# One layer of a graph network: 147 columns and 15 rows of a chunk fetched outside the gather queue instead of 35 columns

## The chip, the core and the metric

The kernel runs on one core of one Trainium2 chip. The metric is the device time of one execution in microseconds (us). Five engines run their own instruction streams and meet at semaphores: PE (matrix products into PSUM; its weight loads are listed as PEld), DVE and ACT (element work on 128 partitions), POOL (here it issues the indirect gathers) and SP (here it issues plain DMAs).

## The reference, cut to what matters

```
def reference(x, src, dst, edge_attr_32, W1, b1, W2, b2):     # 12500 nodes x 48, 400000 edges, dst is sorted
    h   = maximum(layernorm(x), 0)
    tmp = concatenate([h[dst], h[src], edge_attr_32], axis=1)   # 400000 x (48 + 48 + 32)
    msg = relu(tmp @ W1 + b1) @ W2 + b2                         # W1: 128 x 128, W2: 128 x 48
    return x + segment_sum(msg, dst, num_segments=12500)
```

## The kernel before

**Tables.** The product `tmp @ W1` is split by the rows of W1. A first stage (`node_tables`) normalises the nodes and writes two tables of 12500 rows of 128 numbers to DRAM: `tab_a` (the part of `h[dst]`, with the bias) and `tab_b` (the part of `h[src]`). A third copy, `bt`, is `tab_b` turned over and kept on chip: 128 partitions, one column for each node.

**Chunks.** The edges are then worked off in chunks of 1024, each of eight tiles of 128 edges: 390 whole chunks and one of five tiles, 391 in all (`NCH`, `T = 8`). Because `dst` is sorted, all destinations of a chunk lie in a window of `W = 80` nodes. For each chunk:

- `prepare` (L353): SP loads one register (L356) and issues three DMAs: the 80 rows of `tab_a` for the window into `rhs` (L359), the edge attributes into rows 80 to 111 of `lhs` (L364), and the destinations, repeated over 80 partitions, into `row` (L366). POOL gathers one row of `tab_b` for every edge, one indirect DMA for each tile of 128 edges, into `gb` (L373; six buffers, so that POOL runs up to six chunks ahead). DVE makes the one-hot matrix of the destinations in `lhs` (L381, which also sums it up along the edges into `deg`), and a second one, `hot`, with edges on partitions (L388).
- `before` (L394): PE makes `pre[t] = lhs[t] x rhs` for the eight tiles, in PSUM. Every product of float32 numbers shows as two matmuls and two weight loads.
- `hidden` (L411): DVE adds `pre` and `gb` into `hid` (L425), ACT applies relu (L432; L431 for a tile that had no gather).
- `fold` (L435): PE sums `hid[t]` by destination with `hot[t]` into `p_g` (L440), and turns `deg` into the second half of `p_g` (L443). `add` (L446) adds `p_g` into the running segment (L455).
- Every twelve chunks the finished segment is multiplied by W2 and stored (L459 to L487).

**Columns.** One tile now and then is not gathered. Its 128 source rows are copied as columns of `bt` into a tile `gt`, one instruction for each edge (`columns`, L340; the copy is L351), and PE adds `gt` turned over into `pre` (`turned`, L406, L409). The column numbers are loaded from `last` into the copying engine's registers ahead of that (`load`, L328; the load shows as TENSOR_LOAD, L316). `PARTS` says how many a chunk gets: three on DVE, two groups of sixteen on ACT. With 35 a chunk, 106 of the 3125 tiles come this way, and 3019 are gathered.

**Order.** The order of the instructions on each engine is written out by hand (`tc.manual_schedule`, L489 to L537): in turn c, `prepare(c)`, `before(c-1)`, `fold(c-2)`, `turned(c-1)`, `hidden(c-1)`, `add(c-2)`, with ACT's first group of columns ahead of its relu and the second behind it.

Of the kernel before, what the change touches and what calls it, by code (L numbers as in the profile page):

```python
# [22 lines left out]
T = 8  # L23
# [25 lines left out]

COLS = 1  # L50
END = NT // T


PARTS = (
    (True, 0, 3, 1),
    (False, 3, 16, 4),
    (False, 19, 16, 20),
)
PART = sum(n for _, _, n, _ in PARTS)
BASE = 36  # L60
DVE_PARTS = sum(dve for dve, *_ in PARTS)
BEHIND = len(PARTS) - 1

BT0 = 16512
SEG0 = 121888
SEG_SIZE = 8 * L


SEG, NEXT, SEG2 = 40, 41, 42
PLACE0 = 43  # L70
WIDTH = 44
SLOTS = (NCH + 2 + P - 1) // P
# [8 lines left out]

BYCOLS = tiles_of(COLS, PART)
TURNED = {c: [j for j, of in enumerate(BYCOLS) if of == c] for c in set(BYCOLS)}

# [4 lines left out]


def gathered_at(c):

    return [t for t in range(min(T, NT - c * T)) if t not in turned_at(c)]

# [153 lines left out]
def windows(nc, tc, gp, bt, ident, idx, x_t, tab_a, tab_b, dst, edge_t, w1, w2s, b2s, out_t):  # L248


    srci, rel, bw, wrow, last, degs = idx
    with ExitStack() as es:
# [19 lines left out]
        for _, _, n, at in PARTS:  # L272
# [3 lines left out]
            )  # L276
        rows_at = slice(BASE, BASE + 1)
        nc.vector.tensor_scalar(
            last[:, :, rows_at], last[:, :, rows_at], 4 * HID, None, op0=ALU.mult
        )  # L280
        taba8 = tab_a.rearrange("n h -> (n h)").bitcast(U8)

# [19 lines left out]
        st = {}  # L302
        gts = {}

        def group(c):
# [17 lines left out]
        def node(n):  # L323
            return n.with_bounds(min_val=0, max_val=N - 1)

        regs = {}
# [26 lines left out]
        def prepare(c):  # L353
            n = min(T, NT - c * T)
            at = c * CE
            base, = numbers(c, BASE, 1, mybir.EngineType.SP)  # L356
            rhs = rhss[c % 3]
            base = base.with_bounds(min_val=0, max_val=4 * HID * (N - 1))
            nc.sync.dma_start(  # L359
                rhs.bitcast(U8)[:W, :],  # L360
                taba8[bass.ds(base, 4 * HID * W)].rearrange("(w h) -> w h", w=W),
            )
            lhs = ld.tile([P, CE], F32, name="lhs")
            nc.sync.dma_start(lhs[W:K, : n * P], edge_t[:, at : at + n * P])  # L364
            row = ld.tile([W, CE], I16, name="row")
            nc.sync.dma_start(  # L366
                row[:, : n * P],
                dst[at : at + n * P].rearrange("(o e) -> o e", o=1).to_broadcast([W, n * P]),
            )
            st[c] = dict(n=n)  # L370
            gb = gp.tile([P, T, HID], F32, name="gb")
            for t in gathered_at(c):
                nc.gpsimd.indirect_dma_start(  # L373
                    out=gb[:, t, :], out_offset=None, in_=tab_b[:, :],
                    in_offset=bass.IndirectOffsetOnAxis(
                        ap=srci[:, c * T + t : c * T + t + 1], axis=0
                    ),
                )

            deg = degs[c % 3]  # L380
            nc.vector.tensor_scalar(  # L381
                lhs[:W, : n * P], row[:, : n * P], bw[:, c : c + 1], None,
                op0=ALU.is_equal, op1=ALU.add, accum_out=deg[:, :1],
            )
            load(c, 0)
            columns(c, 0)
            hot = wp.tile([P, T, W], F32, name="hot")
            nc.vector.tensor_tensor(  # L388
                hot[:, :n, :], wnum.unsqueeze(1).to_broadcast([P, n, W]),
                rel[:, c * T : c * T + n].unsqueeze(2).to_broadcast([P, n, W]), op=ALU.is_equal,  # L390
            )
            st[c].update(rhs=rhs, lhs=lhs, gb=gb, deg=deg, hot=hot)

# [17 lines left out]
        def hidden(c):  # L411
            s = st[c]
            n, pre = s["n"], s["pre"]
            h = wp.tile([P, T, HID], F32, name="hid")
            two = len(turned_at(c)) == 2
# [8 lines left out]
            to = n - len(turned_at(c))  # L424
            nc.vector.tensor_add(added(h, to), added(pre, to), added(s["gb"], to))  # L425
            if two:
                nc.scalar.activation(
                    h[:, half - 1 :: half, :], pre[:, half - 1 :: half, :], AF.Relu
                )
            elif to < n:  # L430
                nc.scalar.activation(h[:, to, :], pre[:, to, :], AF.Relu)  # L431
            nc.scalar.activation(added(h, to), added(h, to), AF.Relu)  # L432
            s["h"] = h

        def fold(c):  # L435
# [3 lines left out]
            for t in range(n):  # L439
                nc.tensor.matmul(  # L440
                    p_g[:, 0, :], s["h"][:, t, :], s["hot"][:, t, :], start=t == 0, stop=t == n - 1
                )
            nc.tensor.matmul(p_g[:, 1, :], s["deg"], ident[:W, :W], start=True, stop=True)  # L443
            s["p_g"] = p_g
# [44 lines left out]
        with tc.manual_schedule():  # L489
            for c in range(NCH + 2):  # L490
                if c < NCH:
                    prepare(c)
                if c >= NCH:
                    load(c, 0)
# [169 lines left out]
def tile_gnn_preln(  # L664
# [54 lines left out]

    degs = []  # L720
    for k in range(3):
        deg = const.tile([W, P], F32, name=f"deg{k}")
        nc.gpsimd.memset(deg, 0.0)
        degs.append(deg)
    gp = ctx.enter_context(tc.tile_pool(name="gp", bufs=6))
# [76 lines left out]
    with tc.If(outside == 0) as cmp:  # L802
        windows(nc, tc, gp, bt, ident, (srci, rel, bw, wrow, last, degs), x_t, tab_a, tab_b, dst16, edge_t,
                w1, w2s, b2s, out_t)
# [70 lines left out]
```

## Time and profile before

| | |
|---|---|
| runs, median (lowest to highest of 3) | 4821.73 us (4817.93 to 4830.65) |
| the profiled execution | 4847.12 us |
| its span, first to last instruction | 4845.3 us |
| instructions in the trace | 55629 |
| granted clock of PE, mean | 0.614 |
| busy: PE, POOL, ACT, DVE | 61%, 60%, 40%, 32% |

How to read it: "busy" counts the engine's own instructions, not its register loads, waits and DMA issues. In the groups of instructions, a row has the line, engine, operation, out<-in by the program's names, shapes, count, busy us and mean ns of one, and then the idle time of the engine just before these instructions with what ended it; "issue" stands for idle time that no wait in the profile explains. The timeline merges neighbours of one kind: start, us from first start to last end, engine, line, and a count.

### The profile page before, as it was taken

To read this page: it belongs to the slowest core of one execution; us is meant where nothing else is said; L and a number is where in the kernel's file an instruction comes from. 1 tells how busy PE (TensorE), PEld (TensorE's weight loads), DVE (VectorE), ACT (ScalarE), POOL (GpSimd) and SP (SyncE) were. 2 spreads that over 40 slices of the span, in tenths; PEclk is the share of its full clock that TensorE was granted. 3 is DMA by queue.
4 is the path that set the end of the run, shared out by engine and by line. 5 is a ranking of instruction groups with operands and counts; after the bars stand their busy time and mean duration, and the time that the engine had idled before them with its cause. 6 is when DMAs were issued, how large, how long until landed. Compare 5 with 4: busy or idle time off the path is not lost. (4 is left out here: it accounts for less than half of the span.)

```text
span 4845.3 us, 55629 instructions
## 1 busy us (share of the span) xinstructions
PE 2962.1 (61%) x14064; PEld 2628.5 (54%) x14064; DVE 1534.8 (32%) x3366; ACT 1944.3 (40%) x12976; POOL 2895.0 (60%) x3047
## 2 busy tenths in 40 slices
PE   5565565555667555665556757666566655665656
PEld 3555564455556555655555656555455555554545
DVE  4333323332333232333323333332233332323333
ACT  3344343443334343443443444343344343434443
POOL 5466565565656566665656666656666665656663
PEclk7756656666555655556656565655655566656566
DMA  3422222222222222222222222222222222222222
GB/s 123 145 72 75 75 71 72 73 73 72 75 68 77 72 73 71 76 73 71 76 71 73 77 73 75 73 71 75 73 72 76 72 74 72 76 69 76 74 71 60
DMA packets 199966, 367.73 MB, mean 76 GB/s; under 512 B 69362, under 2 KB 101636, under 8 KB 198356
## 3 DMA queue, kind: packets, MB, share of 16 engines
q0 software_dynamic: 96640, 198.07, 16.4%
q1 hardware_dynamic: 102736, 165.92, 11.5%
q8 instruction: 115, 1.88, 0.2%
q14 instruction: 215, 1.76, 0.1%
q10 hardware_dynamic: 260, 0.10, 0.0%
HBM read 344.35 MB, written 22.07 MB: 76 GB/s over the span
## 5 line engine op out<-in xcount | busy, mean ns | idle before, releaser
L373 POOL DMA_INDIRECT gb<-tab_b,srci x3019 | 2873.3, 952 | 1898.0 <-DVE seg L455 953.0
L351 ACT COPY gt<-bt 128x1 f32 x12404 | 1495.6, 188 | 1985.4 <-issue 1957.3
L400 PE MATMUL pre<-rhs,lhs 112*128 112x128 f32 x6250 | 1357.6, 386 | 866.3 <-issue 655.1
L400 PEld LDWEIGHTS pre<-rhs,lhs 112*128 112x128 f32 x6250 | 1240.2, 292 | 1052.9 <-issue 849.9
L440 PE MATMUL p_g<-hot,hid 128*128 128x80 f32 x6250 | 1210.5, 366 | 691.2 <-ACT hid L432 312.9
L440 PEld LDWEIGHTS p_g<-hot,hid 128*128 128x128 f32 x6250 | 1156.3, 280 | 742.8 <-ACT hid L432 351.3
L425 DVE TENSOR_TENSOR hid<-pre,gb 128x1024 f32<-128x1024 f32 (+1 forms) x391 | 461.4, 1180 | 1727.0 <-issue 1357.5
L432 ACT ACTIVATE hid<-hid 128x1024 f32<-128x1024 f32 (+1 forms) x391 | 400.3, 1024 | 423.3 <-DVE hid L425 318.2
L381 DVE TENSOR_SCALAR_CACHE_REDUCE lhs<-row,bw 80x1024 f32<-80x1024 int16 x391 | 495.4, 1267 | 9.3 <-DMA row<-in_dst 9.3
L455 DVE TENSOR_TENSOR seg<-seg,p_g 128x160 f32 x391 | 122.4, 313 | 977.1 <-remote 824.1
L388 DVE TENSOR_TENSOR hot<-wnum,rel 128x640 f32<-128x640 f32 x391 | 316.1, 809 | 0.0
L443 PE MATMUL p_g<-ident,deg 80*128 80x80 f32 x782 | 213.4, 356 | 139.1 <-issue 138.8
L443 PEld LDWEIGHTS p_g<-ident,deg 80*128 80x128 f32 x782 | 181.1, 278 | 111.8 <-issue 111.4
L483 DVE TENSOR_TENSOR xseg<-xseg,p_f 48x512 f32<-48x512 f32 (+1 forms) x67 | 45.3, 676 | 497.6 <-remote 291.2
L431 ACT ACTIVATE hid<-pre 128x128 f32<-128x128 f32 x106 | 29.4, 278 | 390.0 <-DVE hid L425 273.8
L409 PE MATMUL pre<-ident,gt 128*128 128x128 f32 x212 | 70.1, 399 | 106.0 <-issue 96.1
L409 PEld LDWEIGHTS pre<-ident,gt 128*128 128x128 f32 x212 | 51.7, 282 | 108.8 <-issue 98.5
L482 PE MATMUL p_f<-seg,b2s 1*48 1x512 f32 (+1 forms) x134 | 98.0, 810 | 11.8 <-issue 11.8
L481 PE MATMUL p_f<-seg,w2s 128*48 128x512 f32 (+1 forms) x134 | 98.0, 815 | 11.3 <-issue 10.0
L351 DVE COPY gt<-bt 128x1 f32 x1164 | 103.0, 141 | 0.0
L482 PEld LDWEIGHTS p_f<-seg,b2s 1*48 1x48 f32 x134 | 13.4, 139 | 92.7 <-issue 91.8
L471 DVE MEMSET seg<- 128x944 f32 x64 | 54.1, 845 | 9.3
(66 smaller groups left out, 327.3 us busy)
## 6 DMA issues: line engine op xcount, KB each, us to landing
row<-in_dst SPq DMA_DIRECT2D x390, 160.0 KB
lhs<-in_edge_t SPq DMA_DIRECT2D x390, 128.0 KB
gb<-tab_b,srci POOLq DMA_INDIRECT x3019
rhs<-tab_a SPq DMA_DIRECT2D x391, 40.0 KB
xseg<-in_x_t SPq DMA_DIRECT2D x33, 192.0 KB
out_x<-xseg SPq DMA_DIRECT2D x33, 192.0 KB
tab_b<-tab SPq DMA_DIRECT2D x3, 1280.0 KB
tab_a<-tab SPq DMA_DIRECT2D x3, 1280.0 KB
```

The lines of the kernel that those rows point to most:

```text
L351: copy(gts[of][:, e : e + 1], bt8[:, bass.ds(at, 4)].bitcast(F32))
L373: nc.gpsimd.indirect_dma_start(out=gb[:, t, :], out_offset=None, in_=tab_b[:, :], in_offset=bass.IndirectOffsetOnAxis(ap=srci[:, c * T + t ...
L381: nc.vector.tensor_scalar(lhs[:W, : n * P], row[:, : n * P], bw[:, c : c + 1], None, op0=ALU.is_equal, op1=ALU.add, accum_out=deg[:, :1],)
L388: nc.vector.tensor_tensor(hot[:, :n, :], wnum.unsqueeze(1).to_broadcast([P, n, W]), rel[:, c * T : c * T + n].unsqueeze(2).to_broadcast([P ...
L400: nc.tensor.matmul(pre[:, t, :], s["lhs"][:K, t * P : (t + 1) * P], s["rhs"][:K, :], start=True, stop=t not in turned_at(c),)
L409: nc.tensor.matmul(st[c]["pre"][:, t, :], gts.pop(j), ident, start=False, stop=True)
L425: nc.vector.tensor_add(added(h, to), added(pre, to), added(s["gb"], to))
L432: nc.scalar.activation(added(h, to), added(h, to), AF.Relu)
L440: nc.tensor.matmul(p_g[:, 0, :], s["h"][:, t, :], s["hot"][:, t, :], start=t == 0, stop=t == n - 1)
L443: nc.tensor.matmul(p_g[:, 1, :], s["deg"], ident[:W, :W], start=True, stop=True)
L455: nc.vector.tensor_add(to, to, s["p_g"])
L482: nc.tensor.matmul(p_f[:, :n], b2s[:1, :], seg[:1, 1, s], start=False, stop=True)
```

## The change

`PARTS` grows from three groups to nine: four on DVE (19, 16, 16 and 20 columns, 71 in all) and five on ACT (16, 16, 16, 16 and 12, 76 in all), each with a register load of its own. In a turn DVE copies 19 columns between the two one-hots, 32 after them, and 20 behind `add`; ACT copies 48 ahead of the relu and 28 behind it. With 147 columns a chunk 446 tiles come by columns, in 57 chunks two of them.

A new path fetches single rows: SP loads fifteen more registers a chunk, and the new function `rows` issues one DMA of one row of `tab_b` (512 bytes) for each, into a tile `gs`; 45 tiles come this way. 2634 tiles are still gathered.

The one-hot at L381 no longer sums along the edges; the degrees come from PE, which multiplies a constant bfloat16 tile (ones in its first column, zeros elsewhere) with the upper halves of the float32 numbers of `hot`, eight products a chunk in place of one of float32. `hidden` adds in place in PSUM (two or three additions in the 45 chunks that have a tile of single rows), and one relu reads all eight tiles from there.

```diff
--- before.py
+++ after.py
@@ -48,27 +48,35 @@
 
 
 COLS = 1
+ROWS0 = 1
 END = NT // T
 
 
 PARTS = (
-    (True, 0, 3, 1),
-    (False, 3, 16, 4),
-    (False, 19, 16, 20),
+    (True, 0, 19, 1),
+    (True, 19, 16, 20),
+    (True, 35, 16, 36),
+    (True, 51, 20, 52),
+    (False, 71, 16, 72),
+    (False, 87, 16, 88),
+    (False, 103, 16, 104),
+    (False, 119, 16, 120),
+    (False, 135, 12, 136),
 )
 PART = sum(n for _, _, n, _ in PARTS)
-BASE = 36
+BASE = 148
+RPART = 15
 DVE_PARTS = sum(dve for dve, *_ in PARTS)
-BEHIND = len(PARTS) - 1
+BEHIND = len(PARTS) - 2
 
 BT0 = 16512
-SEG0 = 121888
+SEG0 = 122592
 SEG_SIZE = 8 * L
 
 
-SEG, NEXT, SEG2 = 40, 41, 42
-PLACE0 = 43
-WIDTH = 44
+SEG, NEXT, SEG2 = 164, 165, 166
+PLACE0 = 167
+WIDTH = 168
 SLOTS = (NCH + 2 + P - 1) // P
 MOST = 32
 
@@ -80,6 +88,7 @@
 
 
 BYCOLS = tiles_of(COLS, PART)
+BYROWS = tiles_of(ROWS0, RPART)
 TURNED = {c: [j for j, of in enumerate(BYCOLS) if of == c] for c in set(BYCOLS)}
 
 
@@ -88,9 +97,14 @@
     return ((), (T - 1,), (T // 2 - 1, T - 1))[len(TURNED.get(c, ()))]
 
 
+def single_at(c):
+
+    return (T - 2 if c in TURNED else T - 1) if c in BYROWS else None
+
+
 def gathered_at(c):
 
-    return [t for t in range(min(T, NT - c * T)) if t not in turned_at(c)]
+    return [t for t in range(min(T, NT - c * T)) if t not in turned_at(c) and t != single_at(c)]
 
 
 EPS = 1e-5
@@ -248,7 +262,7 @@
 def windows(nc, tc, gp, bt, ident, idx, x_t, tab_a, tab_b, dst, edge_t, w1, w2s, b2s, out_t):
 
 
-    srci, rel, bw, wrow, last, degs = idx
+    srci, rel, bw, wrow, last, ones = idx
     with ExitStack() as es:
         seg = es.enter_context(tc.tile_pool(name="segs", bufs=1))
 
@@ -274,11 +288,11 @@
                 last[:, :, at : at + n], last[:, :, at : at + n], 4, BT0,
                 op0=ALU.mult, op1=ALU.add,
             )
-        rows_at = slice(BASE, BASE + 1)
+        rows_at = slice(BASE, BASE + 1 + RPART)
         nc.vector.tensor_scalar(
             last[:, :, rows_at], last[:, :, rows_at], 4 * HID, None, op0=ALU.mult
         )
-        taba8 = tab_a.rearrange("n h -> (n h)").bitcast(U8)
+        tab8, taba8 = (t.rearrange("n h -> (n h)").bitcast(U8) for t in (tab_b, tab_a))
 
         place = PARTS[0][3] - 1
         for a, b in ((place, SEG2), (NEXT, SEG)):
@@ -301,6 +315,7 @@
             rhss.append(rhs)
         st = {}
         gts = {}
+        gss = {}
 
         def group(c):
 
@@ -322,6 +337,19 @@
 
         def node(n):
             return n.with_bounds(min_val=0, max_val=N - 1)
+
+        def rows(c, nodes):
+
+            for k, n in enumerate(nodes):
+                e = (c - ROWS0) * RPART + k
+                of = BYROWS[e // P]
+                if of not in gss:
+                    gss[of] = gtp.tile([P, HID], F32, name="gs")
+                n = n.with_bounds(min_val=0, max_val=4 * HID * (N - 1))
+                nc.sync.dma_start(
+                    gss[of].bitcast(U8)[e % P : e % P + 1, :],
+                    tab8[bass.ds(n, 4 * HID)].rearrange("(o h) -> o h", o=1),
+                )
 
         regs = {}
 
@@ -353,7 +381,8 @@
         def prepare(c):
             n = min(T, NT - c * T)
             at = c * CE
-            base, = numbers(c, BASE, 1, mybir.EngineType.SP)
+            m = max(0, min(RPART, len(BYROWS) * P - (c - ROWS0) * RPART)) if c >= ROWS0 else 0
+            base, *nodes = numbers(c, BASE, 1 + m, mybir.EngineType.SP)
             rhs = rhss[c % 3]
             base = base.with_bounds(min_val=0, max_val=4 * HID * (N - 1))
             nc.sync.dma_start(
@@ -367,7 +396,7 @@
                 row[:, : n * P],
                 dst[at : at + n * P].rearrange("(o e) -> o e", o=1).to_broadcast([W, n * P]),
             )
-            st[c] = dict(n=n)
+            st[c] = dict(n=n, rows=nodes)
             gb = gp.tile([P, T, HID], F32, name="gb")
             for t in gathered_at(c):
                 nc.gpsimd.indirect_dma_start(
@@ -377,10 +406,8 @@
                     ),
                 )
 
-            deg = degs[c % 3]
             nc.vector.tensor_scalar(
-                lhs[:W, : n * P], row[:, : n * P], bw[:, c : c + 1], None,
-                op0=ALU.is_equal, op1=ALU.add, accum_out=deg[:, :1],
+                lhs[:W, : n * P], row[:, : n * P], bw[:, c : c + 1], None, op0=ALU.is_equal,
             )
             load(c, 0)
             columns(c, 0)
@@ -389,7 +416,7 @@
                 hot[:, :n, :], wnum.unsqueeze(1).to_broadcast([P, n, W]),
                 rel[:, c * T : c * T + n].unsqueeze(2).to_broadcast([P, n, W]), op=ALU.is_equal,
             )
-            st[c].update(rhs=rhs, lhs=lhs, gb=gb, deg=deg, hot=hot)
+            st[c].update(rhs=rhs, lhs=lhs, gb=gb, hot=hot)
 
         def before(c):
 
@@ -411,7 +438,6 @@
         def hidden(c):
             s = st[c]
             n, pre = s["n"], s["pre"]
-            h = wp.tile([P, T, HID], F32, name="hid")
             two = len(turned_at(c)) == 2
             half = T // 2
 
@@ -422,14 +448,17 @@
                 return x.rearrange("p (b t) h -> p b t h", b=2)[:, :, : half - 1, :]
 
             to = n - len(turned_at(c))
-            nc.vector.tensor_add(added(h, to), added(pre, to), added(s["gb"], to))
-            if two:
-                nc.scalar.activation(
-                    h[:, half - 1 :: half, :], pre[:, half - 1 :: half, :], AF.Relu
-                )
-            elif to < n:
-                nc.scalar.activation(h[:, to, :], pre[:, to, :], AF.Relu)
-            nc.scalar.activation(added(h, to), added(h, to), AF.Relu)
+            at = single_at(c)
+            if at is None:
+                parts = [(added(pre, to), added(s["gb"], to))]
+            else:
+                runs = [(0, half - 1), (half, at)] if two else [(0, at)]
+                parts = [(pre[:, a:b, :], s["gb"][:, a:b, :]) for a, b in runs]
+                parts.append((pre[:, at, :], gss.pop(c)))
+            for of, rows in parts:
+                nc.vector.tensor_add(of, of, rows)
+            h = wp.tile([P, T, HID], F32, name="hid")
+            nc.scalar.activation(h[:, :n, :], pre[:, :n, :], AF.Relu)
             s["h"] = h
 
         def fold(c):
@@ -440,7 +469,11 @@
                 nc.tensor.matmul(
                     p_g[:, 0, :], s["h"][:, t, :], s["hot"][:, t, :], start=t == 0, stop=t == n - 1
                 )
-            nc.tensor.matmul(p_g[:, 1, :], s["deg"], ident[:W, :W], start=True, stop=True)
+            high = s["hot"].bitcast(BF16)
+            for t in range(n):
+                nc.tensor.matmul(
+                    p_g[:, 1, :], ones, high[:, t, 1::2], start=t == 0, stop=t == n - 1
+                )
             s["p_g"] = p_g
 
         def add(c):
@@ -490,6 +523,7 @@
             for c in range(NCH + 2):
                 if c < NCH:
                     prepare(c)
+                    rows(c, st[c].pop("rows"))
                 if c >= NCH:
                     load(c, 0)
                     columns(c, 0)
@@ -717,11 +751,9 @@
     flag = const.tile([1, 1], I32, name="flag")
     last = const.tile([P, SLOTS, WIDTH], I32, name="last")
 
-    degs = []
-    for k in range(3):
-        deg = const.tile([W, P], F32, name=f"deg{k}")
-        nc.gpsimd.memset(deg, 0.0)
-        degs.append(deg)
+    ones = const.tile([P, P], BF16, name="ones")
+    nc.gpsimd.memset(ones, 0.0)
+    nc.gpsimd.memset(ones[:, :1], 1.0)
     gp = ctx.enter_context(tc.tile_pool(name="gp", bufs=6))
 
     with tc.tile_pool(name="keep", bufs=1) as keep, tc.tile_pool(
@@ -800,7 +832,7 @@
     outside = nc.values_load(flag[:1, :1], min_val=0, max_val=1)
 
     with tc.If(outside == 0) as cmp:
-        windows(nc, tc, gp, bt, ident, (srci, rel, bw, wrow, last, degs), x_t, tab_a, tab_b, dst16, edge_t,
+        windows(nc, tc, gp, bt, ident, (srci, rel, bw, wrow, last, ones), x_t, tab_a, tab_b, dst16, edge_t,
                 w1, w2s, b2s, out_t)
     with cmp.Else():
         general(nc, tc, bt, ident, x_t, tab_a, tab_b, src_it, dst_it, dst, edge_t, w1, w2s, b2s,
@@ -837,6 +869,10 @@
     cols = np.pad(cols, (0, -len(cols) % PART)).reshape(-1, PART)
     for _, k, n, at in PARTS:
         numbers[COLS : COLS + len(cols), at : at + n] = cols[:, k : k + n]
+    in_rows = [c * T + single_at(c) for c in BYROWS]
+    rows = by_tile[in_rows].reshape(-1)
+    rows = np.pad(rows, (0, -len(rows) % RPART)).reshape(-1, RPART)
+    numbers[ROWS0 : ROWS0 + len(rows), BASE + 1 : BASE + 1 + RPART] = rows
     last = np.ascontiguousarray(numbers.reshape(SLOTS, P, WIDTH).transpose(1, 0, 2))
 
     arrays = {
```

## The prediction

> **What bounds the kernel now.** The page comes first, then the groups of instructions with shapes kept apart.
>
> ```profile
> span 4845.3 us, 55629 instructions
> PE 2962.1 (61%) x14064; PEld 2628.5 (54%) x14064; DVE 1534.8 (32%) x3366; ACT 1944.3 (40%) x12976; POOL 2895.0 (60%) x3047
> ...
> L373 POOL DMA_INDIRECT gb<-tab_b,srci x3019 | 2873.3, 952 | 1898.0 <-DVE seg L455 953.0 <-issue 855.9 <-DVE hid L425 52.6
> L351 ACT COPY gt<-bt 128x1 f32 x12404 | 1495.6, 188 | 1985.4 <-issue 1957.3 <-DVE last L290 4.2
> ```
>
> No engine is full. POOL comes nearest: its gathers and the fixed gap behind each take (2873.3 + 855.9) / 3019 = 1.235 us, or 9.54 us a chunk over 391 chunks, and it waits 953.0 / 391 = 2.44 us a chunk for DVE to free a buffer. The first and last addition of `hidden` give the pace:
>
> ```profile
> L425 DVE TENSOR_TENSOR hid<-pre,gb x391: 809/1209/1226, 157.6 to 4832.7; 128x1024 f32<-128x1024 f32 x140, 128x896 f32<-128x896 f32 x55, 128x640 f32<-128x640 f32 x1
> ```
>
> (4832.7 - 157.6) / 390 = 11.99 us a chunk: gathers plus wait, 9.54 + 2.44. So the other engines are not hidden behind POOL; POOL stops for them. Why they are late is in the waits, where the largest sum of all is not a wait for another engine:
>
> ```profile
> ACT gt L351 <- issue: 1957.3, 2796, 1.9
> ```
>
> 2796 times a column copy came 1957.3 / 2796 = 0.70 us late with nothing to wait for. The timeline says when:
>
> ```profile
> 2003.67 2.55 ACT L351 COPY gt<-bt 128x1 f32 x25
> ...
> 2017.75 0.19 ACT L351 COPY gt<-bt 128x1 f32 x1 [1.20 <-issue]
> ...
> 2019.03 0.94 POOL L373 DMA_INDIRECT gb<-tab_b,srci  x1 [0.30 <-issue]
> 2019.15 0.19 ACT L351 COPY gt<-bt 128x1 f32 x1 [1.21 <-issue]
> 2019.17 0.37 PE L400 MATMUL pre<-rhs,lhs 112*128 112x128 f32 x1 [2.41 <-issue]
> 2019.86 0.19 ACT L351 COPY gt<-bt 128x1 f32 x1 [0.52 <-issue]
> ...
> 2020.57 0.37 PE L400 MATMUL pre<-rhs,lhs 112*128 112x128 f32 x1 [1.03 <-issue]
> ...
> 2025.78 0.95 POOL L373 DMA_INDIRECT gb<-tab_b,srci  x1 [4.55 <-DVE seg L455]
> ...
> 4800.69 0.95 POOL L373 DMA_INDIRECT gb<-tab_b,srci  x1 [0.31 <-issue]
> ...
> 4802.58 3.27 ACT L351 COPY gt<-bt 128x1 f32 x32
> ```
>
> While POOL has been gathering for some microseconds, ACT and PE issue one instruction each 0.7 or 1.4 us; once it pauses they run freely, and behind the very last gather (4800.69) ACT makes 32 copies in 3.27 us, 0.102 us each. Two windows cut one cycle, just over two chunks with 15 gathers, into these halves for ACT's copies:
>
> ```profile
> 2006.10:2024.00 17.90, 4.47 (x29) 0.60 0.21 54
> 2024.00:2029.10 5.10, 3.60 (x37) 0.50 0.40 117
> ```
>
> Slow: 29 copies in 17.9 us, 1.62 per us, and 17.9 / 15 = 1.193 us of slow time a gather. Free: 37 copies in 5.1 us. I read the kernel as two phases that take turns: POOL's gathers, in which the others crawl, and its pause, in which they catch up.
>
> The rule must give the present time. With 3019 / 391 = 7.72 gathers a chunk: slow 9.21 us, in it 14.9 copies of the 12404 / 391 = 31.7; the other 16.8 at 0.102 us take 1.71 us; then the relu, which follows them on ACT:
>
> ```profile
> L432 ACT ACTIVATE hid<-hid 128x1024 f32<-128x1024 f32 x284 | 299.7, 1055 | 415.4 <-DVE hid L425 310.3 <-issue 104.8
> ```
>
> 9.21 + 1.71 + 1.06 = 11.98 us, where 11.99 were measured. ACT's column copies fill the pause already now.
>
> **The change, part by part.**
>
> *Gathers.* 2634 instead of 3019, 6.74 a chunk. Slow time 6.74 x 1.193 = 8.04 us, 1.17 us less: a gain of 390 x 1.17 = 456 us.
>
> *ACT's columns.* 76 instead of 31.7. In the slow 8.04 us go 13.0; the other 63.0 take 63.0 x 0.102 = 6.43 us of pause. The 0.102 us holds the register loads, since the 32 copies are two groups of sixteen with their loads. The pause is then 6.43 + 1.06 = 7.49 us, and the chunk 8.04 + 7.49 = **15.53 us**, 3.54 us more than now.
>
> *DVE's columns.* 71 instead of 3, in order with its other work:
>
> ```profile
> 2026.85 0.27 DVE L351 COPY gt<-bt 128x1 f32 x3
> ...
> L425 DVE TENSOR_TENSOR hid<-pre,gb 128x1024 f32<-128x1024 f32 x284 | 345.2, 1216 | 985.9 <-issue 895.6 <-ACT gt L351 50.9 <-remote 39.3
> L381 DVE TENSOR_SCALAR_CACHE_REDUCE lhs<-row,bw 80x1024 f32<-80x1024 int16 x390 | 494.5, 1268 | 9.3 <-DMA row<-in_dst 9.3
> L388 DVE TENSOR_TENSOR hot<-wnum,rel 128x640 f32<-128x640 f32 x390 | 315.6, 809 | 0.0
> L455 DVE TENSOR_TENSOR seg<-seg,p_g 128x160 f32 x391 | 122.4, 313 | 977.1 <-remote 824.1 <-PE pre L400 53.7 <-issue 53.6
> ...
> L351 DVE COPY gt<-bt 128x1 f32 x1164 | 103.0, 141 | 0.0
> ...
> L316 ACTq TENSOR_LOAD <-last x776: 314/1041/2327, 139.6 to 4811.2; - x194
> L316 DVEq TENSOR_LOAD <-last x425: 315/349/770, 155.6 to 4832.4; - x142
> ```
>
> Copies follow each other at (0.27 - 0.14) / 2 = 0.065 us; the large operations take 1.22 + 1.27 + 0.81 + 0.31 = 3.61 us a chunk. How DVE crawls with columns to make no row shows; I take ACT's rate, 13 copies, which leaves 58 x 0.065 = 3.8 us. Four loads of 16 to 20 numbers cost between DVE's 0.349 us (four numbers or one) and ACT's 1.041 us (sixteen) each, 1.4 to 4.2 us, hidden behind queued copies or not. At most half of the large work, 1.8 us, falls into the slow time. DVE's pause thus lies between 3.8 + 3.6 - 1.8 = 5.6 and 3.8 + 3.6 + 4.2 = 11.6 us. Sixteen copies with their load at ACT's pace, 1.63 us, are nearest: 58 / 16 x 1.63 + 3.6 - 1.8 = 7.7 us, level with ACT's 7.5. I add nothing, and keep both ends.
>
> *Rows by SP.* Fifteen more DMAs a chunk and a load of sixteen numbers.
>
> ```profile
> 2003.45 0.33 SPq L359 DMA_DIRECT2D rhs<-tab_a  x1
> 2003.87 0.37 SPq L364 DMA_DIRECT2D lhs<-in_edge_t  x1
> 2004.29 0.46 SPq L366 DMA_DIRECT2D row<-in_dst  x1
> ```
>
> One issue each 0.42 us: 18 x 0.42 + 1.04 = 8.6 us of the 15.5. Queued behind the rows are the next chunk's `rhs`, `lhs` and `row`, on which PE and DVE wait. Cost nothing while SP gets at least part of the slow time; if it got none, 8.04 + 8.6 = 16.6 us, 1.1 us a chunk more.
>
> *Degrees, one-hot, relu.*
>
> ```profile
> 2003.65 3.70 PE L440 MATMUL p_g<-hot,hid 128*128 128x80 f32 x16 [0.24 <-issue]
> ...
> L443 PE MATMUL p_g<-ident,deg 80*128 80x80 f32 x782 | 213.4, 356 | 139.1 <-issue 138.8
> L431 ACT ACTIVATE hid<-pre 128x128 f32<-128x128 f32 x106 | 29.4, 278 | 390.0 <-DVE hid L425 273.8 <-issue 110.6 <-DVE seg L455 5.6
> ```
>
> L381 loses its sum: a gain between 0 and half of its 1.27 us. On PE two matmuls a chunk (782 / 391) go and eight come, and 446 turned tiles instead of 106 add 1.7; at 3.70 / 16 = 0.23 us each as the upper end and nothing as the lower for the eight, PE is between 0.1 us less and 1.8 us more busy a chunk. ACT's longer pause hides that; uncovered it costs 1.8 us. One relu for all tiles saves L431's 29.4 us, below 0.1 us a chunk. The sum in PSUM keeps a buffer of `pre` until ACT's relu has read it, not only until DVE has added; the next user of that buffer on PE, `before` two chunks on, stands behind `fold` of the same chunk, which waits for that relu already, so nothing is queued behind a new wait. I book all of this at zero.
>
> The Trainium skill, "SBUF — State Buffer", section "Who interferes with whom", says that a `tensor_scalar` without an accumulator output may take a two-port mode that locks GpSimd out, which the present form of L381 does not. No run here shows that form. As an estimate from that page, the halved time would take up to 0.6 us a chunk from DVE and could hold POOL as long.
>
> **Sum.** 390 x 15.53 + 157.6 (first addition) + 4845.3 - 4832.7 (what follows the last) = 6227 us of span. The profiled execution is 1.8 us longer than its span (4847.1) and 25.4 us above the median of the runs (4821.7): 6227 + 1.8 - 25.4 = **6200 us**.
>
> **The rivals.**
>
> *Faster: the columns do hide beside the gathers.* If the 0.70 us delays came from these queues having little ready, a queue full of copies would keep its pace through the gathers. A chunk then takes the busiest engine: POOL 6.74 x 1.235 = 8.3 us, ACT 76 x 0.102 + 1.06 = 8.8, SP 8.6, DVE 71 / 16 x 1.63 + 3.6 = 10.8. 390 x 10.8 + 170 - 24 = **4360 us**, 3580 us with DVE's loads hidden and ACT the bound (8.8). It decides at break-even: a chunk of 11.99 us needs 47.7 of the 76 copies in the slow 8.04 us, 5.9 per us instead of 1.62. Against it stand the 2796 delays with nothing waited for, and PE, whose matmuls were ready and crawled alike. The Trainium skill's page "SBUF — State Buffer", same section, takes this side: "PE and ACT never wait on anyone", and a DMA never contends with a compute engine. These rows do not agree with it, unless the cause lies outside that memory. Chance 0.13.
>
> *Milder:* part of the copies use the slow time better, or fewer gathers in a run leave them freer. At 5 per us: 8.04 + 35.8 x 0.102 + 1.06 = 12.75 us, 5120 us. Chance 0.11, for 4900 to 5600 us.
>
> *DVE is the later one:* its loads stand open: 11.6 - 1.8 = 9.8 us of pause, 17.8 us a chunk, **7090 us**. For it: DVE's copies, loads and large operations are one queue, and `hidden` stands behind 51 copies. Chance 0.20, for 6700 to 7600 us. More than that (both ends together, 19.6 us) 0.05.
>
> **How the numbers follow.** The forecast, 5600 to 6700 us around 6200, has 0.51. The range 5000 to 7600 us leaves out the faster rival, a little of the milder one, and the far end, 2 in 10. A difference of 0.3% is about what the runs can tell from none. Slower 0.86, same 0.01, faster 0.13.
>
> **What would show it.** In the changed profile: 2634 gathers still 1.24 us apart; POOL's wait for DVE up from 2.4 to about 7 us a chunk; the delays before ACT's copies still near 0.70 us, now with DVE's copies showing them too; free stretches of some 7 us with ACT at 0.1 us a copy. I am wrong in the mechanism if copies run at 0.1 us through long runs of gathers, and wrong in size if DVE or SP, not ACT, works last in the pauses.

## The result, and the profile after

The changed kernel takes 5369.16 us (median of 4 runs, 5364.9 to 5372.86) where the kernel before, run beside it, takes 4826.19 us: a ratio of 1.1126 with a 95% interval of 1.1105 to 1.1147, 543 us slower. The forecast (6200 us, 1378 us above the kernel before) had the sign and the two phases, at two and a half times the size.

The page of the changed kernel and its groups of instructions:

```profile
span 5368.5 us, 117719 instructions
PE 3296.4 (61%) x17087; PEld 2982.2 (56%) x17087; DVE 3216.3 (60%) x29465; ACT 3501.3 (65%) x29954; POOL 2588.0 (48%) x2661
...
L379 ACT COPY gt<-bt 128x1 f32 x29488 | 3117.8, 188 | 1675.4 <-issue 1645.1
L402 POOL DMA_INDIRECT gb<-tab_b,srci x2634 | 2566.6, 974 | 2712.3 <-DVE pre L459 1794.2 <-issue 704.5 <-DVE seg L488 169.8
L379 DVE COPY gt<-bt 128x1 f32 x27600 | 2039.7, 145 | 1773.3 <-issue 1751.8 <-DMA gs<-tab_b 3.7
```

The chain of work that ended last, by engine (the profile follows it back through the last 40% of the span):

```profile
DVE 21%; issue 14%; DVEq 2%; ACT 2%; PE 1%; SPq 0%; ACTq 0%; DMA 0%
```

Gathers are still (2566.6 + 704.5) / 2634 = 1.242 us apart. POOL's waits for DVE grew from 2.6 to (1794.2 + 169.8) / 391 = 5.0 us a chunk, where the forecast had some 7, and the delays with nothing to wait for now stand in front of DVE's copies too. The chain is DVE's: its addition, behind which POOL's buffer comes free, stands behind its columns. The list of waits adds how often each came (us in total, times, longest):

```profile
DVE gt L379 <- issue: 1751.8, 3086, 1.3
ACT gt L379 <- issue: 1645.1, 2927, 4.2
...
POOL gb L402 <- DVE pre L459: 1794.2, 350, 54.6
...
POOL gb L402 <- DVE seg L488: 169.8, 28, 7.3
```

The same two waits of POOL in the kernel before:

```profile
POOL gb L373 <- DVE seg L455: 953.0, 217, 8.9
...
POOL gb L373 <- DVE hid L425: 52.6, 11, 48.4
```

The counts hold much of the answer, and the forecast had read only the sums. Before, POOL stopped 217 + 11 = 228 times, so a run of gathers was 3019 / 228 = 13.2 long on average, mostly two chunks. After, it stopped 350 + 28 = 378 times: runs of 2634 / 378 = 7.0, one chunk each. The windows of ACT's copies over one cycle of the changed kernel (length, busy time, instructions, granted clock, DMA share, GB/s) show what a short run does:

```profile
2502.40:2509.80 7.40, 6.20 (x63) 0.65 0.26 68
2509.80:2516.00 6.20, 1.92 (x14) 0.60 0.20 53
```

The free stretch is 7.4 us, where the forecast had 7.49 for ACT's pause; but POOL stands still for only 4.61 us of it, and the rest lies beside the first gathers. The slow one is 6.2 us and not 8.04: the timeline has the first of seven gathers at 2506.06, with ACT making 24 copies at full pace beside the second and third, the last at 2513.72, and ACT free again from 2516.02:

```profile
2506.06 0.94 POOL L402 DMA_INDIRECT gb<-tab_b,srci  x1 [4.61 <-DVE pre L459]
...
2507.79 2.31 ACT L379 COPY gt<-bt 128x1 f32 x24
...
2511.76 0.28 ACT L379 COPY gt<-bt 128x1 f32 x2 [1.14 <-issue]
...
2513.72 0.94 POOL L402 DMA_INDIRECT gb<-tab_b,srci  x1 [0.30 <-issue]
...
2516.02 1.02 ACT L379 COPY gt<-bt 128x1 f32 x10 [0.51 <-issue]
```

So the crawl began 2509.80 - 2506.06 = 3.7 us behind the restart and was over at 2516.02. The same delay stood in the cycle from which the forecast took its rate. Its slow window began at 2006.10, and POOL had restarted 3.3 us earlier:

```profile
2002.78 0.94 POOL L373 DMA_INDIRECT gb<-tab_b,srci  x1 [4.61 <-DVE seg L455]
```

In both cycles these free microseconds came once for the run of gathers, whether it had seven or fifteen.

### The profile page after: what moved, and what is told of

It reads as the page before. It is cut to its first block, busy times and chain, and to the rows that moved or that the text cites. A ratio compares the mean times of both kernels' runs of the same rounds, so it can differ in the third digit from the quotient of the medians.

```text
span 5368.5 us, 117719 instructions
## 1 busy us (share of the span) xinstructions
PE 3296.4 (61%) x17087; PEld 2982.2 (56%) x17087; DVE 3216.3 (60%) x29465; ACT 3501.3 (65%) x29954; POOL 2588.0 (48%) x2661
## 5 line engine op out<-in xcount | busy, mean ns | idle before, releaser
L379 ACT COPY gt<-bt 128x1 f32 x29488 | 3117.8, 188 | 1675.4 <-issue 1645.1
L402 POOL DMA_INDIRECT gb<-tab_b,srci x2634 | 2566.6, 974 | 2712.3 <-DVE pre L459 1794.2
L379 DVE COPY gt<-bt 128x1 f32 x27600 | 2039.7, 145 | 1773.3 <-issue 1751.8
L469 PE MATMUL p_g<-hot,hid 128*128 128x80 f32 x6250 | 1420.8, 420 | 1980.7 <-ACT hid L461 1298.9
L461 ACT ACTIVATE hid<-pre 128x1024 f32<-128x1024 f32 x391 | 396.1, 1013 | 95.9 <-DVE pre L459 76.8
L459 DVE TENSOR_TENSOR pre<-pre,gb 128x896 f32<-128x896 f32 (+2 forms) x394 | 412.7, 1047 | 4.1 <-issue 1.9
L436 PE MATMUL pre<-ident,gt 128*128 128x128 f32 x892 | 329.5, 483 | 24.1 <-remote 21.2
L474 PEld LDWEIGHTS <-ones 128*128 128x128 bf16 x3125 | 295.6, 155 | 0.0
L409 DVE TENSOR_SCALAR lhs<-row,bw 80x1024 f32<-80x1024 int16 x391 | 290.0, 742 | 8.3 <-DMA row<-in_dst 8.3
L474 PE MATMUL p_g<-hot,ones 128*128 128x80 bf16 x3125 | 287.0, 267 | 0.0
```

The source lines that it names most:

```text
L379: copy(gts[of][:, e : e + 1], bt8[:, bass.ds(at, 4)].bitcast(F32))
L402: nc.gpsimd.indirect_dma_start(out=gb[:, t, :], out_offset=None, in_=tab_b[:, :], in_offset=bass.IndirectOffsetOnAxis(ap=srci[:, c * T + t ...
L409: nc.vector.tensor_scalar(lhs[:W, : n * P], row[:, : n * P], bw[:, c : c + 1], None, op0=ALU.is_equal,)
L436: nc.tensor.matmul(st[c]["pre"][:, t, :], gts.pop(j), ident, start=False, stop=True)
L459: nc.vector.tensor_add(of, of, rows)
L461: nc.scalar.activation(h[:, :n, :], pre[:, :n, :], AF.Relu)
```

## The experiments

Columns, rows, degrees and gathers were first taken apart; then, since none of them alone explained the size, the gathers' rhythm was changed. Times are medians, and a ratio stands to the kernel before, run beside it (4824 to 4848 us). The code shows what each edit is about; lines that only follow from it (places in `last`, sizes, the filling of the tables) are left out.

**Do gathers cause the crawl?** The same buffers, zeroed once, and no gather at all, in both kernels:

```
-            for t in gathered_at(c):
-                nc.gpsimd.indirect_dma_start(...)
+        gb = gp.tile(...); nc.vector.memset(gb, 0.0)      # once, ahead of the loop
```

> The changed kernel without its 2634 gathers: one buffer of zeros takes the place of gb, all else stays. Two phases (gathers make the other queues crawl, the rest runs in POOL's pauses): the chunk shrinks from 13.3 us to the free part alone, ACT 76 x 0.102 + 1.0 = 8.8 us, DVE with its loads 8 to 10.8 us: 9.5 us a chunk, about 3870 us (3600 to 4400), and the 0.57 us delays before the copies are gone. Rival, DVE and ACT are simply full of small instructions and the gathers do not matter to them: 13 us a chunk, 5000 to 5370 us, delays still there.

> The kernel before without its 3019 gathers, zeros in their place. Two phases: what is left is PE's two rows of sixteen products, 4 to 8 us a chunk by the granted clock, about 6.5 us: 2700 us (1900 to 3300), no 0.70 us delays. Rival (the gathers only occupy POOL): the others' pace of 11 to 12 us a chunk stays, 4400 to 4800 us.

Measured 3538 us for the changed kernel, a little less than expected, and 2029 us for the one before (one run each). ACT's copies in the groups of the kernel before without gathers:

```profile
L353 ACT COPY gt<-bt 128x1 f32 x12404 | 1223.3, 187 | 24.9 <-issue 10.2 <-DVE last L290 4.2
```

10.2 us of delays where there were 1957.3: the crawl is the gathers'. Without them the change costs 1509 us, the work that it adds.

**The columns alone, from the other side.** All 106 column tiles of the kernel before are gathered instead:

```
-    (True, 0, 3, 1), (False, 3, 16, 4), (False, 19, 16, 20),
+    (True, 0, 0, 1), (False, 0, 0, 4), (False, 0, 0, 20),
```

> The kernel before with no columns at all: all 3125 tiles gathered, DVE and ACT copy nothing. Two phases: 8 gathers a chunk, run together as now, slow about 8.7 us, and the pause loses the 16.8 copies that ACT makes in it (1.7 us of 3.6): 10.6 to 11.5 us a chunk, 4300 to 4650 us, faster than before. Rival, POOL is the bound and every tile taken from it pays: 106 more gathers at 1.235 us are 131 us more, 4950 us.

5119.24 us, a ratio of 1.0605 (1.0586 to 1.0624): slower. The first 106 tiles by columns gain 291 us, 2.7 us a tile, more than the 1.235 us that a gather takes of POOL. So the rule that columns are paid in POOL's pause does not hold for the first of them. The chain and the stops say more:

```profile
PE 48%; issue 45%; another core or an unknown queue 4%; DVE 1%; ACT 1%; DMA 0%; DVEq 0%; SPq 0%; ACTq 0%
```

Without any columns PE and its unexplained delays are the chain, and to take ACT's copies away does not shorten the chunk. POOL stopped 129 + 6 times for DVE, so runs were 3125 / 135 = 23 gathers long, against 13 in the kernel before. That fits a cost that grows with the run; what lengthened the runs was not tried.

**The changed kernel with 35 columns**, rows, degrees and relu as changed:

```
-PARTS = ((True, 0, 19, 1), (True, 19, 16, 20), ... (False, 135, 12, 136))
+PARTS = ((True, 0, 3, 1), (False, 3, 16, 4), (False, 19, 16, 20))
```

> The changed kernel with the columns of the kernel before (3 on DVE, 32 on ACT); rows by SP, degrees by PE, the sum in PSUM with one relu and the one-hot without its sum stay. If the columns carry the loss, this is within 2% of the kernel before, 4650 to 4900 us, a little under it for 45 gathers fewer (56 us) and 0.5 us a chunk less on DVE. Rival, the rows by SP or the eight products for the degrees carry a good part: 5050 us or more.

5588.76 us, a ratio of 1.1565 (1.1545 to 1.1585): slower than with 147. The group of the comparison on DVE names the place:

```profile
L403 DVE TENSOR_SCALAR lhs<-row,bw 80x1024 f32<-80x1024 int16 x391 | 299.1, 765 | 2323.4 <-DMA row<-in_dst 2044.3
```

DVE waits 2044 us for the load of `row`, which stands behind the rows on SP. To see each part by itself, four kernels followed.

**Rows alone** in the kernel before, 45 tiles fewer gathered:

```
                     prepare(c)
+                    rows(c, st[c].pop("rows"))
```

> The kernel before with the fifteen rows a chunk by SP and nothing else of the change (45 tiles no longer gathered; 35 columns, degrees and relu as before). Theory now: SP's queue crawls through the fifteen one-row DMAs beside the gathers and holds back the next chunk's `row`, `lhs` and `rhs` behind it; with everything else as before that alone takes 5350 to 5600 us, and DVE waits for the DMA of `row`. Rival (the degrees on PE carry the loss of the 35-column form): the rows cost nothing and save 45 gathers of 1.2 us, 4750 to 4850 us. As on record before the change, the rows would cost nothing.

5638.22 us, a ratio of 1.1678 (1.1631 to 1.1724). The timeline (start, length, queue or engine, operation, count, idle before) of SP and POOL shows why:

```profile
2498.76 0.41 SPq L389 DMA_DIRECT2D row<-in_dst  x1
2499.27 17.43 SPq L343 DMA_DIRECT2D gs<-tab_b  x15
2517.31 0.32 SPq L382 DMA_DIRECT2D rhs<-tab_a  x1
2517.74 0.36 SPq L387 DMA_DIRECT2D lhs<-in_edge_t  x1
2518.14 0.42 SPq L389 DMA_DIRECT2D row<-in_dst  x1
2518.96 4.88 SPq L343 DMA_DIRECT2D gs<-tab_b  x15
...
2513.24 0.95 POOL L396 DMA_INDIRECT gb<-tab_b,srci  x1 [0.30 <-issue]
2524.38 0.95 POOL L396 DMA_INDIRECT gb<-tab_b,srci  x1 [10.19 <-DVE seg L486]
```

Fifteen rows leave in 4.88 us in POOL's pause (2514.2 to 2524.38) and in 17.43 us beside its gathers, and the next chunk's `row` waits behind them; DVE waits 3206 us for it in all. That is 810 us of loss where nothing was booked.

**Degrees alone** in the kernel before:

```
-                op0=ALU.is_equal, op1=ALU.add, accum_out=deg[:, :1],
+                op0=ALU.is_equal,
...
-            nc.tensor.matmul(p_g[:, 1, :], s["deg"], ident[:W, :W], start=True, stop=True)
+            for t in range(n):
+                nc.tensor.matmul(p_g[:, 1, :], ones, high[:, t, 1::2], start=t == 0, stop=t == n - 1)
```

> The kernel before with the degrees by PE from a column of ones (eight bf16 matmuls a chunk instead of two, the comparison of `lhs` without its sum) and nothing else of the change. Theory now (rows carry the loss): within 100 us of the kernel before, 4780 to 4930 us. Rival (PE's sixteen more queued instructions a chunk crawl beside the gathers): 5250 to 5600 us.

4844.34 us, a ratio of 1.0028 (1.0006 to 1.005): as good as nothing, as booked, with each gather a little longer (952 ns before):

```profile
L373 POOL DMA_INDIRECT gb<-tab_b,srci x3019 | 2991.2, 991 | 1781.6 <-DVE seg L457 824.3
```

The delays before ACT's copies fell here from 1957 to 812 us, and ACT waited longer for DVE's addition in their place. The time did not move, so these delays alone are no price.

**147 columns alone** (the kernel before with the `PARTS` of the changed one):

> The kernel before with 147 columns a chunk (71 DVE, 76 ACT) instead of 35 and nothing else of the change: 340 tiles no longer gathered. Going from 0 to 106 tiles by columns brought 2.7 us a tile; in the changed kernel 340 more brought 0.65 us a tile. Theory now (columns gain, rows lose): 4200 to 4650 us, faster. Rival, the theory on record (columns are made in POOL's pause and cost more than their gathers): 5400 us or more.

5207.31 us, a ratio of 1.0782 (1.0765 to 1.08): 379 us, between the two numbers expected, so both theories had it wrong: the columns do lose, and far less than forecast. **The changed kernel without its rows:**

```
-BYROWS = tiles_of(ROWS0, RPART)
+BYROWS = []
```

> The changed kernel without the rows by SP: their 45 tiles are gathered by POOL again, the 147 columns, the degrees on PE and the one relu in PSUM stay. Theory now (rows carry the loss): faster than both, 4250 to 4700 us. Rival (the degrees on PE or the sum in PSUM carry it): 5150 to 5400 us, about as the changed kernel.

5012.31 us, a ratio of 1.0375 (1.0358 to 1.0392), again between the two. With 147 columns alone POOL stopped 333 + 45 times for DVE, so 2679 gathers came in runs of 7.1. With 35 columns and the rest of the change the runs were 2974 / (193 + 40) = 12.8. So it is the 147 columns that cut them. Taken in this order the parts give the change as a sum: before 4828, columns + 379 = 5207, degrees and relu - 195 = 5012, rows + 357 = 5369; alone in the kernel before, degrees and rows cost 16 and 810 us. The 195 us are DVE's for the most part, as far as the profile tells (degrees and relu were not tried apart with 147 columns): the chain has DVE at 51% with the columns alone and at 25% behind that, and the comparison of `lhs` takes 0.58 of its time without its sum. The chain by engine and L387 with the columns alone, then L409 without rows:

```profile
DVE 51%; issue 32%; ACT 9%; DVEq 3%; PE 1%; ACTq 1%; POOL 0%; DMA 0%; POOLq 0%
...
L387 DVE TENSOR_SCALAR_CACHE_REDUCE lhs<-row,bw 80x1024 f32<-80x1024 int16 x391 | 494.5, 1265 | 7.8 <-DMA row<-in_dst 7.8
```

```profile
L409 DVE TENSOR_SCALAR lhs<-row,bw 80x1024 f32<-80x1024 int16 x391 | 289.1, 739 | 8.5 <-DMA row<-in_dst 8.5
```

391 x (1.265 - 0.739) = 206 us. The one relu is busy for 396 us on ACT, where the relus with the columns alone took 470.

**Longer runs of gathers.** If short runs are why the loss was smaller than forecast, long ones must bring it back. One buffer for two chunks, three of them instead of six:

```
-            gb = gp.tile([P, T, HID], F32, name="gb")
+            if c % 2 == 0:
+                pair[0] = gp.tile([P, 2 * T, HID], F32, name="gb")
+            gb = pair[0][:, c % 2 * T : c % 2 * T + T, :]
```

> The changed kernel with one gather buffer for two chunks (three of them instead of six single ones), so that POOL's gathers come in runs of some 14 instead of 6 to 7; nothing else differs. In the traces the others crawl from 3.7 us after POOL restarts to the end of the run, 6.2 us for a run of 7 but 17.6 us for one of 15. Theory (slow time grows faster than the run, so short runs are why the changed kernel lost less than forecast): slow 16.4 us per two chunks, in it some 27 to 37 of ACT's 152 copies, and (152 - 32) x 0.102 + 2.1 = 14.3 us of pause: 30.7 us per two chunks, 5700 to 6200 us. Rival (slow time per gather does not hang on the run): within 100 us of the changed kernel's 5369 us.

6210.17 us, a ratio of 1.2799 (1.2758 to 1.2839), just above the range expected, where the prediction of the change had been 6200. POOL's stops, the delays before ACT's copies in the whole run, and a window of ACT's copies over one run of fourteen and the start of the pause behind it:

```profile
POOL gb L405 <- DVE pre L462: 2714.6, 185, 62.7
ACT gt L380 <- issue: 2391.8, 3094, 4.2
```

```profile
2508.50:2524.50 16.00, 2.76 (x17) 0.72 0.17 50
2524.50:2535.00 10.50, 8.91 (x92) 0.50 0.11 34
```

Runs of 2634 / (185 + 4) = 13.9 (four more stops were for DVE's `seg`), 16.0 us of slow time for one of fourteen (1.14 us a gather against 0.89 in the run of seven; 1.06 copies per us), ACT free behind it. The same 2634 gathers and 29488 copies now come with 2392 us of delays instead of 1645, and POOL waits 2714.6 / 391 = 6.9 us a chunk. The kernel still has its rows, whose fifteen DMAs also meet longer runs here, so the 10 us between 6210 and 6200 say less than the slow time does.

**Shorter runs and wider gaps.** A dummy write of POOL, which nothing reads, behind the fourth tile of a chunk, or behind every gather (no rows in these two):

```
                 nc.gpsimd.indirect_dma_start(out=gb[:, t, :], ...)
+                if t == 3:                          # first kernel
+                    for _ in range(4): nc.gpsimd.memset(idle, 0.0)
+                nc.gpsimd.memset(idle[:, :384], 0.0)   # second kernel
```

> The changed kernel without the rows, and with four dummy writes of 640 numbers by POOL (some 2.4 us) behind the fourth tile of each chunk, which cut a run of seven gathers into two of three or four. Theory (the crawl starts only 3.7 us behind POOL's restart): most of the slow 6 us a chunk goes, 4200 to 4700 us, where the kernel without rows took 5012. Rival (the others crawl whenever gather packets flow): POOL's longer run adds to it, 5000 to 5500 us.

> The changed kernel without the rows, and with one dummy write of 384 numbers by POOL (some 0.4 us) behind every gather: gathers 1.6 instead of 1.24 us apart. Theory A (the crawl is a backlog that gathers build up at their full rate): 4300 to 4800 us. Theory B (the others crawl as long as gather packets flow, at whatever rate): slow time grows with POOL's time by 2.6 us a chunk, 5200 to 5700 us. Without the dummy writes it took 5012 us.

4726.38 us (0.9748, 0.9717 to 0.9778), just outside the range expected, and 4601.32 us (0.949, 0.946 to 0.9519): faster than the kernel before, and 286 and 411 us faster than without the dummy work. The delays before ACT's copies fell from 1374 us to 1087 and 807 us with the same gathers and the same bytes. So a good part of the slowing hangs on gathers following each other at full rate, and not on their being there.

**Fewer columns**, again without rows:

```
+PARTS = ((True, 0, 19, 1), (True, 19, 16, 20), (False, 35, 16, 36), (False, 51, 16, 52))
```

> The changed kernel without the rows and with 67 columns a chunk (35 by DVE, 32 by ACT) instead of 147; degrees on PE and one relu in PSUM stay. Theory (the first columns, made where an engine has nothing else to do, gain; those beyond that lengthen POOL's pause): 4550 to 4800 us, faster than before. Rival (a straight line between the 4844 us of 35 columns with degrees on PE and the 5012 us of 147): 4890 us.

5102.45 us, a ratio of 1.0524 (1.0491 to 1.0558): both numbers missed. Its waits explain it after the fact:

```profile
POOL gb L397 <- DVE seg L483: 875.4, 130, 12.6
...
POOL gb L397 <- DVE pre L454: 440.3, 87, 52.9
```

2922 / (130 + 87) = 13.5: with 67 columns POOL still runs through two chunks at a time, and pays for the columns as well. That its runs are the reason wasn't tried by itself.

**Gaps in the kernels themselves, and their width.** The changed kernel with its rows and 384, the kernel before with 256, and 512 without rows:

```
+                nc.gpsimd.memset(idle[:, :384], 0.0)   # or :256, :512
```

> The changed kernel as it is, with the rows, and with the dummy write of 384 numbers by POOL behind every gather. Theory 1 (what the rows cost, 357 us, is that their queue and the others crawl beside gathers at full rate): with the crawl thinned out the rows cost little, 4500 to 4750 us. Theory 2 (the rows cost by themselves, as fifteen more transfers and their queue time on SP): 357 us more than the 4601 us of the same kernel without rows, 4900 to 5050 us.

> The kernel before with a dummy write of 256 numbers by POOL (some 0.3 us) behind every gather and nothing else. POOL then needs 7.72 x 1.53 = 11.8 us a chunk of the 12.0 it has. Theory (gathers at their full rate build up a backlog that lets all queues crawl): the others keep their pace and POOL bounds the kernel, 4550 to 4780 us, faster. Rival (spacing helps only where an engine has 76 columns to make): 4830 to 5200 us.

> The changed kernel without the rows, with a dummy write of 512 instead of 384 numbers by POOL behind every gather. POOL's own time is then 6.85 x 1.70 = 11.6 us a chunk. Theory (a wider gap takes more of the 807 us of delays before ACT's copies away, and then POOL bounds): 4450 to 4750 us with delays before ACT's copies below 500 us. Rival (the delays that are left do not hang on the gap): delays of about 800 us still, and 4700 to 4900 us.

4559.93 us (0.9448, 0.9422 to 0.9473), 4700.23 us (0.9736, 0.9712 to 0.976) and 4625.62 us (0.958, 0.9558 to 0.9603). The kernel before gains too, so gaps do not pay only where there are many columns. With gaps of 384 the rows no longer cost: 4560 us with them, 4601 without. Their 357 us came with the gathers at full rate. At 512 the crawl is gone and POOL is the bound (the chain by engine, and groups):

```profile
POOL 82%; issue 10%; DVE 4%; PE 2%; DMA 1%; DVEq 0%; ACT 0%; POOLq 0%; SPq 0%; ACTq 0%
...
L403 POOL DMA_INDIRECT gb<-tab_b,srci x2679 | 2611.4, 975 | 464.1 <-issue 438.5
L380 ACT COPY gt<-bt 128x1 f32 x29488 | 2889.3, 187 | 102.9 <-issue 40.5
...
L409 POOL MEMSET idle<- 1x512 f32 x2679 | 1462.9, 546 | 42.2 <-DMA tab_a<-tab 42.2
```

**Is it the transfers or the indirect form?** In the kernel before, each gather becomes a plain load of 128 neighbouring rows on POOL's queue:

```
-                nc.gpsimd.indirect_dma_start(out=gb[:, t, :], in_=tab_b[:, :], in_offset=...)
+                nc.gpsimd.dma_start(gb[:, t, :], tab_b[at_t : at_t + P, :])
```

> The kernel before with each gather replaced by a plain load of 128 neighbouring rows on the same queue of POOL, same bytes into the same buffer; the sums over edges are then of other rows. Theory A (the crawl comes from transfers of POOL's queue following each other at full rate, indirect or not): POOL's issues stay near 1 us each and the kernel near 4500 to 5000 us, with the 0.7 us delays before ACT's copies. Theory B (it comes from the indirect form): no such delays, 2000 to 3500 us.

2013 us (one run). Its page:

```profile
q0 software_dynamic: 96640, 198.07, 35.1%
...
L374 POOL DMA_DIRECT2D gb<-tab_b x3019 | 1592.8, 536 | 345.4 <-DVE seg L451 166.7
L351 ACT COPY gt<-bt 128x1 f32 x12404 | 1223.3, 187 | 25.4 <-issue 10.0
```

The same 3019 transfers and 198 MB, each issued in 536 instead of 952 ns, and 10.0 us of delays. So neither the bytes nor the number of transfers on POOL's queue make the crawl. Whether the making of an indirect transfer does it or its scattered rows isn't told apart by this run.

**The version that beats both**, the changed kernel with 448, and one step past it, with 179 columns and 480:

```
+                nc.gpsimd.memset(idle[:, :448], 0.0)   # or :480
```

> The changed kernel as it is, with the rows, and with a dummy write of 448 numbers by POOL behind every gather, between the 384 (4560 us, ACT bound with 802 us of delays) and the 512 (4626 us without rows, POOL bound with 40 us of delays). POOL's own time is 6.74 x (0.985 + 0.48 + 0.155) = 10.9 us a chunk, 4410 us in all. Theory (delays end where POOL leaves enough of a gap): 4400 to 4540 us, ACT's delays below 400 us. Rival (the two bounds meet flatly): 4540 to 4600 us, no better than 384.

> The changed kernel with 179 columns a chunk (95 by DVE, 84 by ACT) instead of 147 and a dummy write of 480 numbers by POOL behind every gather; rows and the rest stay. 6.49 gathers a chunk x (0.985 + 0.51 + 0.155) = 10.7 us of POOL; ACT 84 x 0.102 + 1.06 = 9.6 us and DVE about 9.8 us. Theory (without delays the columns go beside the gathers, and fewer gathers pay): 4250 to 4450 us. Rival (DVE or ACT with its register loads becomes the bound): 4550 to 4900 us.

With 448 the changed kernel takes 4391.17 us, a ratio of 0.9107 (0.9078 to 0.9135); its groups:

```profile
L380 ACT COPY gt<-bt 128x1 f32 x29488 | 2930.9, 187 | 204.4 <-issue 127.4
L403 POOL DMA_INDIRECT gb<-tab_b,srci x2634 | 2595.9, 986 | 459.1 <-issue 435.8
...
L409 POOL MEMSET idle<- 1x448 f32 x2634 | 1255.3, 477 | 42.2 <-DMA tab_a<-tab 42.1
```

POOL hardly waits for DVE any more (under 2 us in all), and ACT's delays fell from 1645 to 127 us. With 179 columns and 480 it takes 4610.76 us (0.9547, 0.9511 to 0.9584): not the gain that was expected, since now DVE, with 95 columns and its loads, works last:

```profile
DVE 66%; issue 18%; DVEq 5%; PE 4%; ACT 2%; POOL 1%; DMA 1%; SPq 0%; ACTq 0%; POOLq 0%
```

## Why the prediction was wrong in size

**What held.** The two phases, the engines that crawl, the length of the stretch in which ACT runs freely (7.40 us measured, 7.49 forecast), the copies' 0.1 us in it, 2634 gathers at their old distance. That gathers are the cause is shown by the runs without them. Two of the forecast's own signs did not come: POOL waits 5.0 us a chunk for DVE and not 7, since part of the free stretch lies beside gathers, and the chain names DVE and not ACT as last. ACT waited only 77 us for DVE's addition, so the two queues were nearly level, as the forecast's 7.7 and 7.5 us had them.

**The step that failed: slow time for a gather.** The term 6.74 x 1.193 = 8.04 us took a rate from one run of fifteen and used it for a run of any length. After the change one chunk's seven gathers cost 6.2 us, since the crawl began some 4 us behind POOL's restart, and the change itself cut POOL's runs from 13.2 to 7.0 (the columns alone do it, runs of 7.1; that it is because buffers come free one chunk at a time is read from the waits and was not tried). Put 6.2 us and its 14 copies, which are those of one cycle, into the forecast's sum: 6.2 + 62 x 0.102 + 1.06 = 13.58 us a chunk, 390 x 13.58 + 170 - 24 = 5442 us, 73 us from the 5369 measured. The pairs turn this round: with runs of 13.9 the forecast's number comes out, 6210 us. The agreement of 11.98 with 11.99 us was no evidence for the rate, as that kernel made runs of such a length itself, and it was partly luck: the sum has ACT busy through the whole chunk, while ACT, in the prediction's own lines, stood idle for 390.0 + 415.4 us in front of L431 and L432, 2.1 us a chunk. "ACT's column copies fill the pause already now" is not borne out, since without any columns the kernel is slower. "Fewer gathers in a run leave them freer" stood among the rivals, at 0.11; the list of waits, with 228 stops for 391 chunks, could have priced it.

**Rows, booked at nothing, cost 357 us.** The bound beside it (SP gets nothing in the slow time, 1.1 us a chunk, 430 us) was nearer. Alone in the kernel before they cost 810 us. With gaps of 384 numbers between the gathers the cost is gone.

**Degrees and relu, booked at nothing, gained 195 us** once DVE was late, 0.50 us a chunk of the 0.63 that was the bound for L381. The page "SBUF — State Buffer" of the Trainium skill, section "Who interferes with whom", has `tensor_scalar` without an accumulator output among the operations that can enter a two-port mode; the shorter time, 739 ns for 1265, agrees. That GpSimd would be held shows at most faintly: a gather took 952 ns before and 991 ns with the degrees alone, 0.3 us a chunk, but 957 ns in the pairs, which have the same comparison. The two terms booked at nothing were off in opposite directions, 162 us together, and hid each other.

**The faster rival** needed queues that keep their pace beside gathers. Thinned out by 448 numbers of idle work they do, and the kernel takes 4391 us, near the 4360 of that rival, though with POOL and not DVE as the bound, so that the nearness is chance. What the same section of the Trainium skill's page says, "PE and ACT never wait on anyone", does not describe the gathers at full rate (1957 us of ACT's delays before, 10 us with plain loads); it speaks of the memory's ports, and no run here shows that those are the place.

## What to carry to other kernels

Before a rate of stolen time is carried over to a changed kernel, count how often the engine that steals it stops, not only for how long: the list of waits gives both, and a change that holds buffers longer changes the rhythm as well as the amount. Where all queues slow down beside one engine's transfers, try some idle work between those transfers; here it made 5369 us into 4391 us with nothing else changed. The amount matters, since with too much the spaced engine becomes the bound, as POOL did at 512 numbers. Price each queue that a new transfer is moved onto at its pace beside the gathers (17.4 us for fifteen rows), not at its free one (4.9 us).

## What the hardware showed that was not expected

In the changed kernel the crawl has an edge. Gathers 1.24 us apart put 1645 us of delays before ACT's 29488 copies; (2615.2 + 392.4 + 1085.6) / 2634 = 1.55 us apart 802 us, 1.63 us apart, worked out in the same way, 127 us, and 1.68 us apart (512, without rows) 40 us. With 179 columns 1.64 us apart left 210 us before 32592 copies. The rows for 1.55 us, from the run with 384:

```profile
L380 ACT COPY gt<-bt 128x1 f32 x29488 | 3101.2, 188 | 871.8 <-issue 802.1
L403 POOL DMA_INDIRECT gb<-tab_b,srci x2634 | 2615.2, 993 | 725.5 <-issue 392.4
...
L409 POOL MEMSET idle<- 1x384 f32 x2634 | 1085.6, 412 | 43.0 <-DMA tab_a<-tab 42.2
```

In the kernel before TensorE was also granted a clock of 0.974 without gathers and of 0.985 with plain loads, where it had 0.614 with them; the changed kernel without gathers had 0.782, so gathers are not all that the clock goes by. Why a gather at full rate slows the queues of engines that wait for nothing, and why the crawl begins only behind the first gathers of a run, stays open.
